# Cross attention's output projection: batches 0 with 1 and 2 with 3 in seven block products instead of eight

## The chip, the cores and the metric

The kernel runs on one core of one Trainium2 chip. The metric is the device time of one launch in microseconds (us): the median of three runs. Besides there is one profiled execution, whose trace gives the start and the duration of every instruction on TensorE (PE, matmuls), VectorE (DVE), ScalarE (ACT), GpSimd (POOL) and SyncE (SP, which here issues nearly all DMAs), and the DMA transfers.

## The reference

A decoder of two layers with the norm behind each residual add, in float32, on `x` of 8 batches of 128 tokens with 512 features. It has a self-attention, a cross attention on a context of the same shape, and feed-forward parts with routed experts and low-rank factors. The part that the change touches is the second layer's cross attention. For each batch, cut to what matters:

```python
hidden = concat([ctx, x])                     # 256 rows of 512
q = x @ Wq.T; k = hidden @ Wk.T; v = hidden @ Wv.T   # 16 query heads, 4 key heads, of 96
p = softmax(q @ k.T / sqrt(96))               # four query heads share a key head
o = p @ v                                     # 128 tokens x 1536 features
x = layernorm(x + o @ Wo.T)                   # Wo.T: 1536 x 512
```

The product `o @ Wo.T` is the output projection. Behind it stands the low-rank feed-forward `f1` of the same batch with its own residual add and norm, and the result goes to `out`.

## The kernel before, in words

All work of the last stage (from about 500 us on) is one loop, `for b in range(B): for hh in range(2)`. Each pass works on eight of the 16 heads of one batch:

- `Heads8` issues 48 score matmul instructions (`s_x`), DVE takes the maxima (`m_x`), ACT the exponentials (`e_x`), DVE scales and transposes blocks of 32x32 (`exps`).
- `turn` moves the transposed blocks into place with 16 DMAs of 64 KB on SP's queue, `pT_x<-e_x`. The tile pT has one buffer, so the moves of batch b wait until `o_x` of batch b-1 has read it. `e_x` has two buffers.
- `outputs(b)`, through `mixed`, multiplies by the values: 48 matmul instructions in three groups (`o_x`), each group in a PSUM bank of its own, whose copy to `oT` frees the bank.
- `projected(b)` does the projection, twelve float32 matmuls that are two instructions each, so 24 instructions of 128x512 (`pox`, line 998), with the three weight tiles `w_X_o`, and `add_norm` adds the residual and norms on DVE, with one power on POOL.
- `low_rank(b - 1)` issues steps of the f1 part: `low_tokens` (transposes), `low_scores`, `low_turn` and `low_last` of several batches, each a pass later.

PE's gaps are filled by `Front`: queries, keys and values of the next two batches in 14 pieces; `nxt.go(n)` issues the next n. PE, SP and the other queues run in program order. The order is written out by hand by this loop; the tile framework adds the semaphores. Matmul outputs share four PSUM banks of one tag. The last two batches have an order of their own, with moves on SP's and ACT's queues, and the last projection in two halves of 256 columns (line 1225).

The weight pool has eight slots of 1 MB. The three `w_X_o` tiles (in_X_o0, o1, o2) are loaded at about 462 to 502 us, ahead of the stage:

```python
wos = [weight(f"X_o{i}").rearrange("p (c o) -> p c o", c=4) for i in range(3)]
```

and the pass order around the change is:

```python
if b < B - 2 and hh == 0:
    nxt.go((4, 3)[j] if b < B - 3 else 2)
    if b:
        mix(b - 1)            # outputs(b - 1), projected(b - 1)
    pTs[b] = pT_tile(b)
    now.turn(pTs[b])
```

Of the kernel before, what the change touches and what calls it, by code (L numbers as in the profile page):

```python
# [11 lines left out]
F32 = mybir.dt.float32  # L12
AF = mybir.ActivationFunctionType
ALU = mybir.AluOpType
# [3 lines left out]
P = 128  # L18
B, S, D = 8, 128, 512
# [24 lines left out]
def decoder(ctx: ExitStack, tc: tile.TileContext, a: dict, out: bass.AP):  # L44
    nc = tc.nc

    glob = ctx.enter_context(tc.tile_pool(name="glob", bufs=1))
    xp = ctx.enter_context(tc.tile_pool(name="xp", bufs=10))
    wp = ctx.enter_context(tc.tile_pool(name="wp", bufs=8))
# [13 lines left out]
    def weight(key):  # L63
        src = a[key]
        t = wp.tile([P, 2048], F32, tag="w", name=f"w_{key}")
        n = src.shape[1]
        nc.sync.dma_start(t[:, :n], src)
        return t
# [212 lines left out]
    xs = [None] * B  # L281
# [6 lines left out]
    ap = attn.enter_context(stage("a0", 2))  # L288
# [232 lines left out]
    for n, (p, f) in enumerate(steps):  # L521
# [8 lines left out]
        now = Heads16(ap, units, causal_bias, oTs[p][:, :, f, :], f"a0_{p}_{f}")  # L530
# [244 lines left out]
    ap = layer.enter_context(stage("a1", 2))  # L775
# [10 lines left out]
    NS = XD // 32  # L786
# [65 lines left out]
    for b in range(B):  # L852
        qT, kbd = qk
        v_now = v
        oT = ap.tile([P, NC, P], F32, tag="oT", name=f"oT1_{b}")
        for f in (0, 2):
# [4 lines left out]
            now = Heads16(ap, units, alibi_bias(f), oT[:, f : f + 2, :], f"a1_{b}_{f}", keys_late)  # L861
# [46 lines left out]
    layer.close()  # L908
    for k in ("q0", "q1", "q2"):
        wqs.append(weight4(f"X_{k}"))  # L910
    wos = [weight(f"X_o{i}").rearrange("p (c o) -> p c o", c=4) for i in range(3)]


    with stage("x1b", 2, side="right") as ap, stage("f1", 2, side="right") as fp:
# [9 lines left out]
        class Heads8:  # L924
# [42 lines left out]
            def turn(self, pT, queues=(nc.sync,)):  # L967
                e = self.e.rearrange("p (s j) h k -> p s j (h k)", s=2)
                for i in range(4):
                    for j in range(4):  # L970
                        queues[j % len(queues)].dma_start(
                            pT[32 * j : 32 * j + 32, :, i, self.h0 // 2, :], e[32 * i : 32 * i + 32, :, j, :]
                        )

# [17 lines left out]
        def projection(b, oT, between={}):  # L992

            po = bank(f"pox_{b}")
            for i in range(NX):
                n, h = divmod(i, G)
                w = wos[(h * NS + n) // 4][:, (h * NS + n) % 4, :]
                nc.tensor.matmul(po, lhsT=oT[:, n, h * P : (h + 1) * P], rhs=w, start=(i == 0), stop=(i == NX - 1))  # L998
                for piece in between.get(i, ()):
                    piece()  # L1000
            return po

        def turned_low(b):
            xT = fp.tile([P, NC, P], F32, tag="xT", name=f"xTf1_{b}")
# [72 lines left out]
        nxt, upcoming = Front(1), None  # L1077
        tokens_low, scores_low, turned_lows = {}, {}, {}

        def low_tokens(b):  # L1080
            tokens_low[b] = turned_low(b)

        def low_scores(b):
            scores_low[b] = scored(b, tokens_low.pop(b))

        def low_turn(b):
            turned_lows[b] = turned_heads(b, scores_low.pop(b))

        def low_last(b):
            last(b, low_sum(b, turned_lows.pop(b)))  # L1090

        def low_rank(b):

            if b >= 2:
                low_turn(b - 2)
            if b >= 1:
                low_scores(b - 1)
            low_tokens(b)
            if b >= 2:
                low_last(b - 2)  # L1100

        def pT_tile(b):
            return ap.tile([P, 2, 4, 2, 8 * 32], F32, tag="pT", name=f"pT_x1_{b}", bufs=1)

        pTs, vs_x, oTs_x = {}, {}, {}

        def outputs(b):
            oTs_x[b] = ap.tile([P, NS, 512], F32, tag="oT", name=f"oTx_{b}", bufs=1)
            mixed(b, vs_x.pop(b), pTs.pop(b), oTs_x[b])

        def projected(b, between={}):
            po = projection(b, oTs_x.pop(b), between)
            xs[b] = add_norm(xs[b], po, f"x1_{b}")

        def mix(b):
            outputs(b)
            projected(b)

        for b in range(B):
            pr, j = divmod(b, 2)  # L1120
            if j == 0 and b:
                front, nxt = nxt, upcoming
            toks = slice(j * P, (j + 1) * P)
            for hh in range(2):
                now = Heads8(front.qT[:, :, toks], front.kT[:, :, :, toks], 2 * hh, f"x1_{b}_{hh}")
                now.maxima()
                now.exps(0)
                now.exps(1)
                if b < B - 2 and hh == 0:

                    nxt.go((4, 3)[j] if b < B - 3 else 2)
                    if b:
                        mix(b - 1)
                    pTs[b] = pT_tile(b)
                    now.turn(pTs[b])
                elif b < B - 2:
                    if j == 1 and b < B - 3:

                        upcoming = Front(pr + 2)
                    now.turn(pTs[b])  # L1140
                    nxt.go(2)
                    if b:
                        low_rank(b - 1)
                    if b < B - 3:
                        nxt.go((1, 2)[j])
                elif hh == 0:

                    if b == B - 2:
                        front.go(3)
                    else:  # L1150
                        projected(b - 2)
                    first = now
                else:
                    low_turn(b - 3)
                    outputs(b - 1)
                    if b == B - 2:
                        low_scores(B - 4)
                        low_last(B - 5)
                    else:
                        low_tokens(B - 3)  # L1160

                    pTs[b] = pT_tile(b)
                    for heads in (first, now):
                        heads.turn(pTs[b], (nc.sync, nc.scalar))
            vs_x[b] = front.v[:, j]
# [40 lines left out]
        b = B - 1  # L1206
        oT = oTs_x.pop(b)
# [12 lines left out]
        for half, cols in enumerate(halves):  # L1220
            po = bank(f"pox_{b}_{half}")
            for i in range(NX):
                n, h = divmod(i, G)
# [102 lines left out]
def _rows(w):  # L1326

    return np.ascontiguousarray(w.T.reshape(-1, P, w.shape[0]).transpose(1, 0, 2)).reshape(P, -1)


def _layouts(i):
    x, c = i["x"], i["ctx_4096"]
    xT = x.reshape(B // 2, 2 * P, NC, P).transpose(3, 0, 2, 1)
    cT = c.reshape(B // 2, 2 * S, NC, P).transpose(3, 0, 2, 1)
    wqkv = i["L1_attn_Wqkv"]
    cols = lambda v: v.reshape(NC, P).T
    HG = E0 * R0 // 2
    lora_b = np.zeros((P, 2 * D), np.float32)
    lora_b[:HG] = i["L0_ffn_lora_B"].transpose(0, 2, 1).reshape(2, HG, D).transpose(1, 0, 2).reshape(HG, 2 * D)
    a = {  # L1340
        "x": x,
        "xT": xT,
        "ctx": c,
        "ctxT": cT,
        "masks": _mask_table(),
        "dft": _dft_table(),
        "alibi": _alibi_table(),
        "vecs": np.stack(
            [cols(i[k]) for k in ("L0_attn_bq", "L0_attn_bk")], axis=1
        ),  # L1350
        "L1_lnq": np.stack([cols(i[f"L1_attn_{k}"]) for k in ("q_ln_w", "q_ln_b")], axis=1),
        "L1_ln": np.stack([i[f"L1_attn_{k}"] for k in ("q_ln_w", "q_ln_b", "k_ln_w", "k_ln_b")]),
        "L0_bvo": np.stack([i["L0_attn_bv"], i["L0_attn_bo"]]),
        "F0_base": _rows(i["L0_ffn_base_W"]),
        "F0_lora": np.concatenate(
            [_rows(np.concatenate([i["L0_ffn_gate_W"], i["L0_ffn_lora_A"].reshape(E0 * R0, D)])), lora_b], axis=1
        ),
        "F1": np.concatenate(
            [
                _rows(np.concatenate([i["L1_ffn_Wr"], i["L1_ffn_A"].reshape(H1 * R1, D)])),  # L1360
                i["L1_ffn_B"].transpose(0, 2, 1).reshape(H1 * R1, D),
            ],
            axis=1,
        ),
        "F1_br": i["L1_ffn_br"],
        "L1_Wo": _rows(i["L1_attn_Wout"]),
        "X_v": _rows(i["L1_xattn_Wv"]),
    }
    for n in "qkvo":
        a[f"L0_W{n}"] = _rows(i[f"L0_attn_W{n}"])  # L1370
        if n in "qk":
            a[f"L0_W{n}"] = a[f"L0_W{n}"].reshape(P, NC, NC, P).transpose(0, 2, 1, 3)
    for n, j in zip("qkv", range(3)):
        a[f"L1_W{n}"] = _rows(wqkv[j * D : (j + 1) * D])

    NS = XD // 32
    wq = i["L1_xattn_Wq"].reshape(KV, G, NS, 32, D).transpose(1, 2, 0, 3, 4).reshape(3, 512, D)
    wo = i["L1_xattn_Wo"].reshape(D, KV, G, NS, 32).transpose(0, 2, 3, 1, 4).reshape(D, 3, 512)
    for j in range(3):
        a[f"X_q{j}"] = _rows(wq[j])  # L1380
        a[f"X_o{j}"] = _rows(wo[:, j])
    a["X_k"] = _rows(i["L1_xattn_Wk"].reshape(KV, NS, 32, D).transpose(1, 0, 2, 3).reshape(KV * XD, D))
    return {k: np.ascontiguousarray(v) for k, v in a.items()}

# [17 lines left out]
```

## Time and profile before

| | |
|---|---|
| median of 3 runs | 873.94 us (873.93 to 873.97) |
| profiled execution, its own time | 874.61 us |
| its span | 872.8 us |
| PE busy in the span | 847.6 us (97%) |
| DVE, ACT, POOL busy | 542.3, 365.1, 202.7 us |
| DMA | 50.67 MB, mean 58 GB/s |

The profile's page and the views of the trace count from the start of the span. A line of a view names the engine, the source line (L998 is line 998), the tiles it writes and reads (`pox<-w_X_o,oTx`), the number of instructions (x24), and durations. "SPq" is SP's queue of DMA issues. PEclk is the clock granted to TensorE, 1.00 being full speed. Matmuls overlap, so the busy time of a single one is longer than the distance between two.

### The profile page before, as it was taken

What the parts mean: (1) busy time and instruction counts of PE and PEld (TensorE: products, weight loads), DVE (VectorE), ACT (ScalarE), POOL (GpSimd) and SP (SyncE); (2) the same over time, 40 slices, a digit from 0 to 9 for tenths busy, and PEclk for the clock granted to TensorE, in tenths of its full rate; (3) what the DMA queues carried; (4) which work ended last, traced back from release to release, by engine and by line L of the source; (5) the groups of instructions that cost most, each with busy time, mean ns of one, the idle gap of its engine ahead of it and who ended that gap; (6) DMA issues with size and microseconds to landing.
All of it is one profiled execution on the core that took longest, in us unless ns stands there. A gap on an engine that the chain in (4) does not pass through costs nothing.

```text
span 872.8 us, 17973 instructions
## 1 busy us (share of the span) xinstructions
PE 847.6 (97%) x6482; PEld 525.3 (60%) x6482; DVE 542.3 (62%) x2214; ACT 365.1 (42%) x1527; POOL 202.7 (23%) x299
## 2 busy tenths in 40 slices
PE   9999999999899999999999999999999999999996
PEld 5776655655454455555555587848385846576454
DVE  3656687777868667777778413724372546467654
ACT  3886574654222136766666403304031322224310
POOL 2500243242535314555555300000000000000000
PEclk9999999999999999999999999999999999999999
DMA  9700000130300002000003020432213211313340
GB/s 327 310 2 26 2 13 14 50 110 10 137 13 0 25 0 98 2 2 2 2 3 145 26 74 1 88 82 49 46 36 86 44 46 36 82 41 80 84 93 36
DMA packets 30073, 50.67 MB, mean 58 GB/s; under 512 B 5536, under 2 KB 22048, under 8 KB 28192
## 3 DMA queue, kind: packets, MB, share of 16 engines
q1 hardware_dynamic: 27424, 47.42, 18.0%
q10 hardware_dynamic: 2560, 2.10, 1.1%
q8 instruction: 51, 0.84, 0.4%
q14 instruction: 38, 0.31, 0.1%
HBM read 30.63 MB, written 2.10 MB: 37 GB/s over the span
## 4 chain that ended last, share of the span: by engine, by line
PE 64%; DVE 18%; ACT 11%; POOL 3%; issue 1%; DMA 1%; ACTq 0%; SPq 0%; POOLq 0%; DVEq 0%
PE pqx L86 10%; PE pox L998 7%; ACT e_a L197 7%; PE pkx L86 4%; PE pvx L86 4%; PE s_x L936 4%; PE o_x L981 4%; PE pq L86 3%; PE pk L86 3%; DVE e_a L184 3%; PE pv L86 3%; PE po L86 3%; PE pt_a L228 2%; PE pof L623 2%; PE s_a L165 2%
## 5 line engine op out<-in xcount | busy, mean ns | idle before, releaser
L197 ACT ACTIVATE e_a<-e_a,m_a 128x128 f32<-128x128 f32 (+1 forms) x512 | 184.7, 364 | 98.7 <-DVE m_a L184 98.7
L957 ACT ACTIVATE e_x<-s_x,m_x 128x256 f32<-128x256 f32 x128 | 58.7, 484 | 139.6 <-DVE m_x L947 122.5
L197 ACT ACTIVATION_READ_ACCUMULATOR e_a<-e_a,m_a 128x1 f32 x512 | 97.0, 189 | 0.0
L86 PE MATMUL pqx<-xTx,w_X_q 128*128 128x256 f32 x384 | 84.9, 380 | 0.0
L86 PEld LDWEIGHTS pqx<-xTx,w_X_q 128*128 128x128 f32 x384 | 72.6, 190 | 11.4 <-issue 1.8
L998 PE MATMUL pox<-w_X_o,oTx 128*128 128x512 f32 x168 | 74.1, 596 | 0.7 <-DVE oTx L987 0.6
L97 POOL TENSOR_TENSOR rs_x<-ve_x,neghalf 128x1 f32<-128x1 f32 x7 | 3.9, 550 | 268.5 <-DVE ve_x L95 249.4
L946 DVE TENSOR_REDUCE m_x<-s_x 128x4 f32<-128x1024 f32 x32 | 37.6, 1218 | 41.5 <-PE s_x L936 41.5
L211 POOL TENSOR_TENSOR e_a<-e_a,rc_a 128x512 f32<-128x512 f32 (+1 forms) x64 | 52.8, 847 | 33.8 <-DVE rc_a L208 18.8
L998 PEld LDWEIGHTS pox<-w_X_o,oTx 128*128 128x128 f32 x168 | 31.3, 190 | 40.9 <-issue 39.2
L228 PE MATMUL pt_a<-ident,e_a 128*128 128x128 f32 x384 | 48.4, 273 | 2.3 <-DVE m_a L184 2.3
L936 PE MATMUL s_x<-kTx,qTx 32*128 32x256 f32 x768 | 50.0, 385 | 0.6 <-ACT e_x L957 0.6
L228 PEld LDWEIGHTS pt_a<-ident,e_a 128*128 128x128 f32 x384 | 43.4, 140 | 11.2 <-issue 4.7
L184 DVE CUSTOM_DVE_ANT_0 e_a<-s_a,masks 128x128 f32<-128x128 f32 (+1 forms) x256 | 46.8, 253 | 4.5 <-PE s_a L165 3.1
L936 PEld LDWEIGHTS s_x<-kTx,qTx 32*128 32x128 f32 x768 | 39.0, 184 | 16.7 <-issue 11.7
L184 DVE CUSTOM_DVE_ANT_0 e_a<-s_a,alibi 128x128 f32<-128x128 f32 (+1 forms) x256 | 47.3, 252 | 1.4 <-PE s_a L165 1.3
L981 PE MATMUL o_x<-pT_x,vx 128*32 128x512 f32 x384 | 43.7, 595 | 1.9 <-DVE mv_x L93 0.7
L184 DVE DVE_READ_ACCUMULATOR2_ANT m_a<- 128x1 f32 x512 | 42.5, 83 | 0.0
L965 DVE STREAM_TRANSPOSE e_x<-e_x 128x1024 f32<-128x1024 f32 x32 | 39.7, 1241 | 0.8
L964 DVE TENSOR_SCALAR e_x<-e_x,rc_x 128x256 f32<-128x256 f32 x128 | 36.3, 347 | 3.5 <-DVE rc_x L961 2.3
L165 PEld LDWEIGHTS s_a<-kbd,qT 32*64 32x64 f32 x1024 | 20.9, 131 | 27.9 <-issue 15.4
L103 DVE TENSOR_TENSOR x_x<-pox,x_a 128x512 f32<-128x512 f32 x7 | 4.8, 686 | 52.5 <-PE pox L998 52.5
(236 smaller groups left out, 1625.4 us busy)
## 6 DMA issues: line engine op xcount, KB each, us to landing
pT_x<-e_x SPq DMA_DIRECT2D x224, 64.0 KB, 2.0
w_X_q<-in_X_q SPq DMA_DIRECT2D x3, 1024.0 KB, 4.9
w_X_o<-in_X_o SPq DMA_DIRECT2D x3, 1024.0 KB, 4.9
w_L_Wv<-in_L_Wv SPq DMA_DIRECT2D x2, 1024.0 KB, 6.6
w_L_Wo<-in_L_Wo SPq DMA_DIRECT2D x2, 1024.0 KB, 7.5
x_in<-in_x SPq DMA_DIRECT2D x8, 256.0 KB, 7.5
ct<-in_ctx SPq DMA_DIRECT2D x8, 256.0 KB, 2.7
cT<-in_ctxT SPq DMA_DIRECT2D x4, 512.0 KB, 3.9
```

The lines of the kernel that those rows point to most:

```text
L86: nc.tensor.matmul(ps, lhsT=l, rhs=r, start=(i == 0), stop=(i == n - 1))
L165: nc.tensor.matmul(s[r // 2][64 * u : 64 * u + 64, r % 2, cols], lhsT=qT[rows, 64 - 64 * part : P - 64 * part], rhs=kbd[rows, :, :keys], s ...
L184: self.scored = nc.vector.tensor_tensor_reduce(self.e[:, r, cols], s[i][:, r % 2, cols], bias(r, cols), -1.0, 3e38, ALU.add, ALU.min, self ...
L197: nc.scalar.activation(e[:, r, x, :], e[:, r, x, :], AF.Exp, scale=-1.0, bias=self.m[:, part, r, x : x + 1], accum_out=self.su[:, part, r, ...
L211: nc.gpsimd.tensor_tensor(e, e, bc(self.rc[:, part, rs, :].unsqueeze(3), list(e.shape)), ALU.mult)
L228: nc.tensor.transpose(pt[:, r, cols], self.e[:, 2 * i + r, cols], ident)
L936: nc.tensor.matmul(sc[g // 2][:, g % 2, u * 256 : (u + 1) * 256], lhsT=qT[rows, (h0 + u) * NS + n, :], rhs=kT[rows, n], start=(n == 0), st ...
L946: nc.vector.tensor_reduce(m, self.s[i], AX.X, ALU.max, negate=True)
L957: nc.scalar.activation(self.e[:, :, j, :], self.s[half][:, i, :].rearrange("p (a k) -> p a k", k=32), AF.Exp, bias=self.m[:, j : j + 1], s ...
L965: nc.vector.transpose(self.e[:, :, js, :], self.e[:, :, js, :])
L981: nc.tensor.matmul(po[32 * g : 32 * g + 32, :], lhsT=v[:, s, g * XD + 32 * n : g * XD + 32 * n + 32], rhs=pT[:, s].rearrange("p i h x -> p ...
L998: nc.tensor.matmul(po, lhsT=oT[:, n, h * P : (h + 1) * P], rhs=w, start=(i == 0), stop=(i == NX - 1))
```

## The change

For the batches 0 and 1, and again 2 and 3, the two projections are done together. Stacked, the two batches' `o` is a matrix of two block rows (batches) and two block columns (768 features each), and Wo.T one of two by two blocks of 768 x 256. The product of two by two blocks is formed in seven block products and a number of block sums (Winograd's form) instead of eight products. One block product is six matmuls of 128x256, two instructions each, so a pair has 84 instructions of 128x256 where there were 48 of 128x512. Batches 4 to 7 are projected as before.

- The weight sums: `form_sums` loads three tiles of 1 MB (in_X_ot) behind the moves of batch 0's first half, and POOL forms the sums in place with twelve subtractions of 128x512. `keep_sums`, behind the moves of batch 0's second half, writes them to a tensor `ts` in DRAM (3 MB). The early load of `w_X_o` is gone.
- `stream(t)` loads one slot's worth (1 MB, in one or two DMAs) of blocks and kept sums, in the order in which the products read them. `stream(0)` to `stream(2)` stand behind the moves of batch 1's first half. Inside a pair, after every eight matmuls, the slot just used is loaded anew; `plain_outputs` loads the plain weights behind the second pair.
- In `paired` POOL forms the left sums, ACT copies two products out of PSUM, DVE and POOL add the products and the residual, and both batches are normed.
- `oT` has two buffers. For even b up to 4 the pass has three front pieces, `outputs`, one piece, `paired`; for odd b the projection is missing from the pass.
- The low-rank steps of batches 0 to 4 are issued from a table `LOWS`, later than before, and the tail has `low_turn` and `low_last` of one more batch.

```diff
-    wos = [weight(f"X_o{i}").rearrange("p (c o) -> p c o", c=4) for i in range(3)]
+    slots = [wp.tile([P, 2048], F32, tag="w", name=f"w_X_o_{i}") for i in range(3)]
+    wos = [t.rearrange("p (c o) -> p c o", c=4) for t in slots]
+    kept = ctx.enter_context(tc.tile_pool(name="kept", bufs=1, space=bass.MemoryType.DRAM))
+    weight_sums_kept = kept.tile([P, 4, 3, 512], F32, tag="ts", name="ts")
+    def form_sums():
+        for i, t in enumerate(slots):
+            nc.sync.dma_start(t, a["X_ot"][:, i])
+            b11, b12, b21, b22 = (t[:, j * 512 : (j + 1) * 512] for j in range(4))
+            nc.gpsimd.tensor_tensor(b11, b12, b11, ALU.subtract)
+            nc.gpsimd.tensor_tensor(b12, b22, b12, ALU.subtract)
+            nc.gpsimd.tensor_tensor(b22, b22, b11, ALU.subtract)
+            nc.gpsimd.tensor_tensor(b21, b21, b22, ALU.subtract)
+    def keep_sums():
+        for i, t in enumerate(slots):
+            nc.sync.dma_start(weight_sums_kept[:, :, i, :], t.rearrange("p (j o) -> p j o", j=4))
...
+    BLOCK = 6 * 256
+    ORDER = [B11, T1, B21, T2, B22, T3, T4]
+    def stream(t):
+        lo, hi = 2048 * t, min(2048 * (t + 1), 7 * BLOCK)
+        while lo < hi:
...
+            nc.sync.dma_start(slots[t % 3][:, lo - 2048 * t : lo - 2048 * t + n], source[:, base + off : base + off + n])
+            lo += n
+    def plain_outputs():
+        for i, t in enumerate(slots):
+            nc.sync.dma_start(t, a[f"X_o{i}"])
...
-                        queues[j % len(queues)].dma_start(
+                        self.moved = queues[j % len(queues)].dma_start(
...
+        def paired(b0, b1):
+            o0, o1 = oTs_x.pop(b0), oTs_x.pop(b1)
...
+            def product(left):
+                ps = bank(f"pox_{b0}_{used[0]}")[:, :256]
+                for kk in range(6):
+                    h, n = divmod(kk, NS)
+                    t, u = divmod(used[0], 8)
+                    nc.tensor.matmul(
+                        ps, lhsT=left[:, n, h * P : (h + 1) * P], rhs=slots[t % 3][:, u * 256 : (u + 1) * 256],
+                        start=kk == 0, stop=kk == 5,
+                    )
+                    used[0] += 1
+                    if u == 7:
+                        if t < 3:
+                            stream(t + 3)
+                        elif t < 5 and not paired.last:
+                            stream(t - 3)
+                return ps
+            add(nc.gpsimd, s, o1[:, :, first], o1[:, :, second])
+            add(nc.gpsimd, o1[:, :, first], o0[:, :, first], o1[:, :, first], ALU.subtract)
+            nc.scalar.copy(p1, product(o0[:, :, first]))
+            nc.scalar.copy(p5, product(s))
+            add(nc.gpsimd, s, s, o0[:, :, first], ALU.subtract)
+            add(nc.gpsimd, x0[:, first], x0[:, first], p1)
+            add(nc.vector, r0[:, first], product(o0[:, :, second]), x0[:, first])
+            add(nc.gpsimd, o0[:, :, second], o0[:, :, second], s, ALU.subtract)
+            add(nc.vector, p1, product(s), p1)
+            add(nc.gpsimd, x0[:, second], x0[:, second], p5)
+            add(nc.gpsimd, x0[:, second], x0[:, second], p1)
+            add(nc.vector, r0[:, second], product(o0[:, :, second]), x0[:, second])
+            add(nc.gpsimd, x1[:, second], x1[:, second], p5)
+            add(nc.vector, p1, product(o1[:, :, first]), p1)
+            add(nc.gpsimd, x1[:, first], x1[:, first], p1)
+            add(nc.gpsimd, r1[:, second], x1[:, second], p1)
+            add(nc.vector, r1[:, first], product(o1[:, :, second]), x1[:, first])
+            if paired.last:
+                plain_outputs()
+            else:
+                stream(2)
...
-            oTs_x[b] = ap.tile([P, NS, 512], F32, tag="oT", name=f"oTx_{b}", bufs=1)
+            oTs_x[b] = ap.tile([P, NS, 512], F32, tag="oT", name=f"oTx_{b}", bufs=2)
...
+        PAIRED = 4
+        LOWS = {
+            2: [lt(0), lt(1)],
+            3: [lsc(0), lsc(1)],
+            4: [lh(0), lh(1), lt(2), ll(0), lt(3), ll(1)],
+            5: [lsc(2), lsc(3), lt(4)],
+        }
...
-                    nxt.go((4, 3)[j] if b < B - 3 else 2)
-                    if b:
+                    if b > PAIRED:
+                        nxt.go((4, 3)[j] if b < B - 3 else 2)
                         mix(b - 1)
+                    elif b and not j:
+                        nxt.go(3)
+                        outputs(b - 1)
+                        nxt.go(1)
+                        paired.last = b == PAIRED
+                        paired(b - 2, b - 1)
+                    else:
+                        nxt.go((4, 3)[j])
+                        if b:
+                            outputs(b - 1)
                     pTs[b] = pT_tile(b)
                     now.turn(pTs[b])
+                    if b < 2:
+                        with tc.issue_after(now.moved.ins):
+                            if b:
+                                for t in range(3):
+                                    stream(t)
+                            else:
+                                form_sums()
                 elif b < B - 2:
...
                     now.turn(pTs[b])
+                    if not b:
+                        with tc.issue_after(now.moved.ins):
+                            keep_sums()
                     nxt.go(2)
-                    if b:
-                        low_rank(b - 1)
+                    for piece in LOWS.get(b, ()):
+                        piece()
```

## The prediction

> **What bounds the kernel.** The page first: TensorE (PE) is busy 97% of the span, and its idle time there is small. So what counts is PE work removed, and any place where PE is made to wait.
>
> ```profile
> PE 847.6 (97%) x6482; PEld 525.3 (60%) x6482; DVE 542.3 (62%) x2214; ACT 365.1 (42%) x1527; POOL 202.7 (23%) x299
> ```
>
> Second, the chain of waits for 565 to 660 us (start, us, what; cross attention of batches 0 to 2):
>
> ```profile
> 570.28 5.29 PE o_x L981 x48
> 575.57 10.50 PE pox L998 x24
> ...
> 614.89 1.90 PE o_x L981 x16
> ...
> 617.56 1.97 PE o_x L981 x16
> ...
> 620.24 1.97 PE o_x L981 x16
> ...
> 622.84 10.57 PE pox L998 x24
> ...
> 653.27 6.91 PE pqx L86 x32
> ```
>
> A projection is 24 instructions of 128x512 in 10.50 us: 0.4375 us each. A 128x256 one costs 6.91/32 = 0.216. Batch 1's o_x is cut into three: each third waits until its accumulator's copy has given the one free PSUM bank back.
>
> Third, the timeline of SP's queue (start, us) from 545 to 611 us, in pieces: the moves of each half of pT, the context load between, the halves of batch 1.
>
> ```profile
> 546.12 10.33 SPq L971 DMA_DIRECT2D pT_x<-e_x  x16
> 557.41 10.68 SPq L971 DMA_DIRECT2D pT_x<-e_x  x16
> 568.18 0.53 SPq L800 DMA_DIRECT2D cT<-in_ctxT  x1
> 575.63 10.70 SPq L971 DMA_DIRECT2D pT_x<-e_x  x16
> 598.90 10.67 SPq L971 DMA_DIRECT2D pT_x<-e_x  x16
> ```
>
> Sixteen moves take 10.3 to 10.7 us of SP (0.64 each) and land 2.0 later. The last of batch 0 is issued at 567.5 and lands near 569.5; o_x of batch 0 starts at 570.28, when PE's queries end. The slack is 0.7 us. So SP's queue is the second bound.
>
> Fourth, what large loads and long waits cost: the page's issues, those of 20 to 40 us (four 1 MB loads in a row), and the windows around PE's wait at 225.5 us (us, PE busy, PEclk, DMA, GB/s).
>
> ```profile
> pT_x<-e_x SPq DMA_DIRECT2D x224, 64.0 KB, 2.0
> w_X_o<-in_X_o SPq DMA_DIRECT2D x3, 1024.0 KB, 4.9
> w_L_Wo<-in_L_Wo SPq DMA_DIRECT2D x2, 1024.0 KB, 7.5
> ```
>
> ```profile
> w_F_base<-in_F_base SPq DMA_DIRECT2D x1, 1024.0 KB, 7.8
> w_L_Wk<-in_L_Wk SPq DMA_DIRECT2D x1, 1024.0 KB, 13.2
> ```
>
> ```profile
> 225.50:228.20 2.70, 0.08 (x1) 0.96 0.02 9
> 228.20:229.20 1.00, 0.97 (x5) 0.50 0.00 0
> 229.20:230.20 1.00, 1.00 (x3) 0.50 0.00 0
> ```
>
> A 1 MB load alone lands in 4.9 us. Of four issued 0.67 apart the first lands 7.8 and the last 13.2 after its issue: (13.2+3x0.67-7.8)/3, about 2.5 us per MB. After 2.65 us of idle PE the granted clock was 0.50 until 231.4, 3.4 us.
>
> **What the change removes.** (a) Each of two pairs: 48 instructions of 128x512 (21.0 us) become 84 of 128x256 (84 x 0.2168 = 18.2). Two pairs: -5.6 us.
>
> (b) For even b the order is now three front pieces, `outputs`, one piece, product. The fourth piece held banks; without it two are free. Batch 1's o_x took 622.84-614.82 = 8.02 us; 5.36 are its matmuls and 0.70 moved-up scores, so 1.96 is stall. Batch 3's at 706.6 is the same. I take back 1.96 and 1.1 (there a bank is still held by low-rank work): -3.1; bounds 0 and -3.9.
>
> **What it adds on SP, part one (stall A).** Between batch 0's two groups of moves come three 1 MB loads of `form_sums`, issued 556.5 to 557.8. By the w_X_o row and 2.55 per MB they land near 561.4, 564.0, 566.5. In the changed kernel's order every SP issue waits for the issue eight before it. So move 6 of the second group waits for load 1, move 8 for load 3 (566.5), and moves 9 to 16 follow at 0.64: last issue 571.7, landing 573.7. PE wants it at 570.25: 3.4 us of idle, nothing else being ready on PE, whose queue is in order. Bounds: 0.3 if loads and moves share the engines so well that only three issues (1.9, less the slack and the gap of 1.0 between the groups) are felt; 5.5 if the loads land as at 23 us, first after 7.8. I take 3.4, by the w_X_o row, whose loads are like these in size. The twelve Pool instructions (128x512 with two tensors: 1.27 us, L478) start at 561.4 and end near 577, beside all this; the third write of `keep_sums` waits for them, and behind it on SP stand the context load and batch 1's moves, gated by o_x until 579 anyhow: nothing. After 3.4 us of idle I charge the clock as after 2.65: 3.4 us at half, 1.7 us; bounds 0 and 1.7.
>
> [...]
>
> **Part two (stall B).** Let T be the end of batch 0's o_x. Batch 1's first moves take T to T+10.9, six `stream` loads (3 MB) to T+14.7. The last of these lands near T+20.7 (start T+10.9, fixed part 2.0 as the moves show, 3 x 2.55). The second group's move 8 waits for it; move 16 goes at T+25.9 and lands T+27.9. With the projection gone from this place PE reaches o_x of batch 1 at T+2.8+13.9+2.8+1.0+5.2 = T+25.7 (scores, queries, scores, transposes, two thirds of the values). Stall 2.2 us; the bounds are 1.1, where only the six issues are felt (second group from T+14.7 instead of T+12.9, where its softmax ends), and 5, where the loads land as at 23 us. Without the loads the last move would land at T+25.0, just in time. A clock fall here: 0 to 1.7, at nothing, as 2.2 is under the 2.65 seen.
>
> **Inside a pair.** Pool's subtractions of 128x768 (1.27 x 1.5 = 1.9 us) are chained; the fifth product's left side needs the second product's end (5.2 us into the pair), a subtraction, two 128x256 adds of 0.65 and another subtraction: 5.2+1.9+1.3+1.9 = 10.3, and some 0.3 for semaphores, against the product's start at 10.4. So 0.2 late per pair: 0.4 for both pairs; bounds 0 and 2. A slot is consumed in 8 x 2 x 0.2168 = 3.47 us, so a stream has 6.9 us from issue to use against 4.9 + 0.6: covered with 1.4. Batch 4's o_x is limited by its moves already (0.6 wait before); the pair's DVE work adds 0.7 (bounds 0 and 2).
>
> **Later.** The low-rank steps of batches 0 to 3 move by the LOWS table; their PE work is the same. One more add and norm (f1 of batch 2) falls to DVE in the tail, where the chain runs DVE, ACT's queue, pT, e_x (808.31 to 813.06 us in the trace): add 0.59, statistics 0.70 and scaling 0.55 are 1.8, of which I let 1.0 reach the end, since some of it falls into a wait of 0.65 there; bounds 0 and 2.5. Leaving out the early 3 MB loads at 462 us saves nothing: they hide.
>
> **Sum.** -5.6 -3.1 +3.4 +1.7 +2.2 +0.4 +0.7 +1.0 = +0.7. The profiled execution took 874.6 with a span of 872.8, 0.7 over the median 873.94; a difference of spans carries over: 874.6 us. With each term at its bounds the mechanism holds some 870 to 878.
>
> **Rival 1, faster: the stalls are hidden.** If loads and moves interleave on the DMA engines, A is near 0.3 with no clock fall, and B 1.1: -8.7+0.3+1.1+2.1 = -5.2, so 868.7; with B at 0, 867.6. For it: a move is 64 KB and moves alone use under half the DMA engines (0.41 from 575.6 to 586.1 us). Against: the wait for the issue eight before holds moves whatever their size. It decides at pT landing before 570.3. [...]
>
> **Rival 2, slower: streams late inside the pair.** Place: streams 3 and 4, issued behind a PE release and read 6.9 us later. The w_L_Wo row has 1 MB landing after 7.5, w_F_base 7.8, the next 9.6. With 7.5 to 9.6 the stall is 7.5+0.6-6.9 = 1.2 to 3.3 per pair, 2.4 taken: +4.8, so 879.4. For: the streams come in pieces, partly from the sums in DRAM, and the next 1 MB is issued 3.5 behind. Against: at 2.5 us per MB the engines keep up. It decides at a landing of 6.3.
>
> That the sums bring no saving in PE time at all (128x256 matmuls at more than 0.22) is spoken against by L1225's tail products of that form.
>
> **Chances.** Forecast 0.50 (870 to 878), rival 1 0.20, rival 2 and stalls at their upper bounds 0.30. 0.2% is 1.75 us, about what a measurement can tell. Within the forecast 0.10 of the 0.50 falls under 872.2, 0.22 between, 0.18 above 875.7. Faster 0.30, same 0.22, slower 0.48. The range 867 to 881 leaves out about a tenth at either end.
>
> **What would show it.** Right: the pox products at 0.217 each, 168 of them; PE idle 3 to 4 us before o_x of batch 0 and PEclk 0.5 after it; a second wait of some 2 us before o_x of batch 1; o_x of batches 1 and 3 in one run; SP waits on w_X_o loads ahead of pT moves. Wrong: no PE idle there (rival 1), or pox waiting on a DMA of w_X_o (rival 2), or DVE and Pool slowing each other in the pairs.

## The result, and the profile after

The changed kernel takes 881.23 us (median of 6 runs, 879.55 to 883.60) against 873.96 (873.71 to 874.70): a ratio of 1.0084, interval 1.0068 to 1.0100. It is slower by 7.3 us. The forecast was 874.6 with a range to 881.0, so the time lies just outside. The profiled execution took 881.59, its span is 879.8, 7.0 more than before.

The page first, PE's line and the landing times of the new DMAs:

```profile
PE 843.9 (96%) x6554; PEld 539.8 (61%) x6554; DVE 551.1 (63%) x2220; ACT 366.6 (42%) x1531; POOL 240.8 (27%) x331
```

```profile
w_X_o<-in_X_ot SPq DMA_DIRECT2D x3, 1024.0 KB, 8.2
...
w_X_o<-in_X_ob SPq DMA_DIRECT2D x4, 768.0 KB, 4.6
w_X_o<-ts SPq DMA_DIRECT2D x6, 512.0 KB, 5.5
```

PE's busy time fell by 3.7 us, and yet the span grew by 7.0: PE waits. Where, the timeline of SP's queue tells (start, us):

```profile
556.18 1.56 SPq L917 DMA_DIRECT2D w_X_o<-in_X_ot  x3
557.85 16.86 SPq L1008 DMA_DIRECT2D pT_x<-e_x  x16
574.81 2.86 SPq L926 DMA_DIRECT2D ts<-w_X_o  x3
...
583.34 10.92 SPq L1008 DMA_DIRECT2D pT_x<-e_x  x16
594.31 0.59 SPq L942 DMA_DIRECT2D w_X_o<-in_X_ob  x1
```

Batch 0's second group of moves took 10.68 us of SP before; now it takes 16.86, behind the three loads. The chain of waits for 534 to 700 us goes through just these places:

```profile
557.31 11.69 DMA w_X_o<-in_X_ot
...
574.12 2.01 DMA pT_x<-e_x
...
576.26 7.06 PE o_x L1018 x48
...
596.90 10.47 DMA w_X_o<-ts
...
612.49 2.00 DMA pT_x<-e_x
...
614.69 8.28 PE o_x L1018 x48
...
625.75 18.29 PE pox L1056 x84
```

The third load holds the chain for 11.69 us, then nine moves go out one by one, then o_x starts at 576.26 (before: 570.28), and takes 7.06 us instead of 5.29. The same happens again with the streams and batch 1's moves. PE's waits (total us, times, longest) around batch 0's, batch 1's and batch 4's o_x, and SP's from 555 to 615 us:

```profile
PE o_x L1018 <- DMA pT_x<-e_x: 6.7, 1, 6.7
PE o_x L1018 <- DMA pT_x<-e_x: 5.6, 1, 5.6
PE o_x L1018 <- DMA pT_x<-e_x: 0.7, 1, 0.7
```

```profile
SPq L1008 <- DMA w_X_o<-in_X_ot: 6.7, 2, 3.4
SPq L1008 <- DMA w_X_o<-ts: 4.3, 2, 3.0
```

So SP itself waited 6.7 us for the loads. In the trace the DMAs take eight semaphores in turn, and each of these issues went out only when the DMA eight issues before it had landed: move 6 of the group at 561.05, load 1 having landed at 561.03, move 7 at 565.07 (load 2: 565.05), move 8 at 569.01 (load 3: 569.00). The seven moves issued ahead of that had landed by 570.34, so what o_x waited for is the nine behind. In and behind both stalls the granted clock (last columns: PEclk, DMA share, GB/s) is 0.50, from 572.84 to 579.66 and from 613.80 to 620.62:

```profile
569.00:573.00 4.00, 0.57 (x3) 0.98 0.35 78
573.00:577.00 4.00, 0.74 (x4) 0.50 0.58 162
577.00:581.00 4.00, 4.00 (x32) 0.67 1.03 380
...
613.00:617.00 4.00, 2.31 (x12) 0.60 0.15 33
617.00:621.00 4.00, 4.00 (x24) 0.55 0.00 0
```

The pair itself does what it says: 84 products in 18.29 us and, for the second pair, 18.31, with no wait for weights.

### The profile page after: what moved, and what is told of

Its sections match the earlier page's. It is cut to its first block, busy times and chain, and to the rows that moved or that the text cites. A ratio compares the mean times of both kernels' runs of the same rounds, so it can differ in the third digit from the quotient of the medians.

```text
span 879.8 us, 18232 instructions
## 1 busy us (share of the span) xinstructions
PE 843.9 (96%) x6554; PEld 539.8 (61%) x6554; DVE 551.1 (63%) x2220; ACT 366.6 (42%) x1531; POOL 240.8 (27%) x331
## 2 busy tenths in 40 slices
DMA packets 35258, 67.99 MB, mean 77 GB/s; under 512 B 5984, under 2 KB 22496, under 8 KB 32992
## 4 chain that ended last, share of the span: by engine, by line
PE 55%; DVE 20%; ACT 10%; SPq 5%; DMA 4%; POOL 3%; issue 2%; ACTq 0%; POOLq 0%; DVEq 0%
PE pqx L86 7%; ACT e_a L197 6%; SPq L1008 5%; PE pox L1056 4%; PE o_x L1018 4%; PE pq L86 4%; DVE e_a L184 3%; PE pk L86 3%; PE pv L86 3%; PE po L86 3%; PE s_x L973 3%; PE pkx L86 2%; PE pt_a L228 2%; PE pox L1035 2%; PE pof L623 2%; PE pvx L86 2%
## 5 line engine op out<-in xcount | busy, mean ns | idle before, releaser
L211 POOL TENSOR_TENSOR e_a<-e_a,rc_a 128x512 f32<-128x512 f32 (+1 forms) x64 | 52.8, 846 | 35.1 <-DVE rc_a L208 18.8
L1018 PE MATMUL o_x<-pT_x,vx 128*32 128x512 f32 x384 | 47.6, 646 | 14.1 <-DMA pT_x<-e_x 13.0
L973 PE MATMUL s_x<-kTx,qTx 32*128 32x256 f32 x768 | 46.6, 383 | 0.0
L1001 DVE TENSOR_SCALAR e_x<-e_x,rc_x 128x256 f32<-128x256 f32 x128 | 42.6, 395 | 3.9 <-DMA pT_x<-e_x 2.6
L1018 PEld LDWEIGHTS o_x<-pT_x,vx 128*32 128x32 f32 x384 | 13.3, 117 | 44.0 <-issue 33.6
L843 ACT COPY qTx<-pqx 128x512 f32<-128x512 f32 x24 | 14.2, 592 | 55.9 <-PE pqx L86 55.9
L165 PE MATMUL s_a<-kbd,qT 32*64 32x256 f32 (+1 forms) x1024 | 33.5, 334 | 1.5 <-ACT pT_a L229 1.0
L1048 POOL TENSOR_TENSOR s_x<-oTx 128x768 f32<-128x768 f32 x2 | 3.6, 1810 | 113.1 <-DVE oTx L1024 113.1
```

Of the source, the lines that this page charges most:

```text
L165: nc.tensor.matmul(s[r // 2][64 * u : 64 * u + 64, r % 2, cols], lhsT=qT[rows, 64 - 64 * part : P - 64 * part], rhs=kbd[rows, :, :keys], s ...
L211: nc.gpsimd.tensor_tensor(e, e, bc(self.rc[:, part, rs, :].unsqueeze(3), list(e.shape)), ALU.mult)
L973: nc.tensor.matmul(sc[g // 2][:, g % 2, u * 256 : (u + 1) * 256], lhsT=qT[rows, (h0 + u) * NS + n, :], rhs=kT[rows, n], start=(n == 0), st ...
L1001: nc.vector.tensor_scalar(e, e, self.rc[:, j : j + 1], None, ALU.mult)
L1018: nc.tensor.matmul(po[32 * g : 32 * g + 32, :], lhsT=v[:, s, g * XD + 32 * n : g * XD + 32 * n + 32], rhs=pT[:, s].rearrange("p i h x -> p ...
```

## The experiments

Two theories were tested. **Q**: the loss is made at SP's queue, by moves of pT that stand behind large loads. **P**: the pair itself costs, by Pool and DVE slowing each other, by streams inside the pair, by more DMA traffic.

**Sums early (e1).** The sums' loads and subtractions where the plain weights were loaded before; the rest as changed.

```diff
+    form_sums()                      # behind plain_outputs, ahead of the stage
...
-                    if b < 2:
+                    if b == 1:
                         with tc.issue_after(now.moved.ins):
-                            if b:
-                                for t in range(3):
-                                    stream(t)
-                            else:
-                                form_sums()
+                            for t in range(3):
+                                stream(t)
```

> Weight sums loaded and formed where the plain weights were loaded before (about 462 to 510 us); the writes to DRAM and the streams stay where the change has them. Theory Q (moves of pT held on SP behind the large loads): the wait ahead of batch 0's o_x (6.75 us in the changed kernel) and the half clock after it (1.66) go, the wait ahead of batch 1's o_x (5.7) stays: 881.2 - 8.4 + 0.7 (the shift that the missing early loads gave) = 873.5 us. Rival P (the pair itself costs: Pool and DVE slowing each other, streams inside the pair, more DMA traffic): 879 or more.

Measured 876.22 us (874.10 to 878.83; before 874.24), ratio 1.0023 (1.0012 to 1.0034), 2.7 above the expectation; run e3 below shows where such a loss comes from. Batch 0's wait is gone, batch 1's is there:

```profile
PE o_x L1019 <- DMA pT_x<-e_x: 6.4, 1, 6.4
```

**Streams late (e2).** The first three streams behind batch 1's second group instead of its first.

```diff
-                            if b:
-                                for t in range(3):
-                                    stream(t)
-                            else:
-                                form_sums()
+                            form_sums()          # only for b == 0
...
-                    if not b:
+                    if b < 2:
                         with tc.issue_after(now.moved.ins):
-                            keep_sums()
+                            if b:
+                                for t in range(3):
+                                    stream(t)
+                            else:
+                                keep_sums()
```

> The first three streams moved behind the second group of moves of batch 1, all else as changed. Theory Q: the wait ahead of batch 1's o_x (5.7 us) and the half clock after it (about 1.7) go, that of batch 0 stays: 881.2 - 7.4 = 873.8 us, with o_x of batch 1 some 1.2 shorter still if its copies then keep up. Rival P: 879 or more, or the first product now waits for its weights (then 876).

Measured 875.02 us (874.12 to 875.80), ratio 1.0007 (0.9998 to 1.0016), 1.2 above the expectation; 0.6 of it is a longer wait ahead of batch 4's o_x (1.3 against 0.7 in the changed kernel). Now batch 1's wait is gone and batch 0's stands:

```profile
PE o_x L1018 <- DMA pT_x<-e_x: 6.8, 1, 6.8
```

**Both (e3).** The two edits together.

> Both edits: sums formed early, first streams behind the second group of moves of batch 1. Theory Q: both waits gone, 881.2 - 8.4 - 7.4 + 0.7 = 866.1 us, 0.991 of before: the saving of 5.2 in the products and of 1 to 2 in the thirds of o_x is then seen. Rival P: 875 or more.

Measured 868.57 us (868.30 to 868.72), ratio 0.9935 (0.9920 to 0.9950). Neither large wait is left; of waits for pT there is only batch 4's:

```profile
PE o_x L1019 <- DMA pT_x<-e_x: 0.9, 1, 0.9
```

This is theory Q: the same pairs, the same 3 MB of sums and the same streams inside the pairs, and 12.7 us less. It is 2.5 above the expectation. The timeline of POOL (this kernel, then one line of the kernel before) and PE's windows of 465 to 500 us (us, busy; this kernel, then the kernel before) tell where:

```profile
466.81 1.27 POOL L674 TENSOR_TENSOR k<-k,lnv 128x512 f32<-128x512 f32 x1 [1.33 <-DVE k L672]
468.05 1.27 POOL L919 TENSOR_TENSOR w_X_o<-w_X_o 128x512 f32<-128x512 f32 x1
469.29 1.26 POOL L675 TENSOR_TENSOR k<-k,lnv 128x512 f32<-128x512 f32 x1
...
471.86 1.27 POOL L921 TENSOR_TENSOR w_X_o<-w_X_o 128x512 f32<-128x512 f32 x1
473.08 1.61 POOL L211 TENSOR_TENSOR e_a<-e_a,rc_a 128x512 f32<-128x512 f32 x2
```

```profile
469.57 1.61 POOL L211 TENSOR_TENSOR e_a<-e_a,rc_a 128x512 f32<-128x512 f32 x2
```

```profile
465.00:500.00 35.00, 32.36 (x350) 1.00 0.16 58
```

```profile
465.00:500.00 35.00, 34.40 (x375) 1.00 0.17 60
```

The subtractions (L919 to L921) stand between Pool's steps for self-attention (L674, L675, L211), which before followed each other; e_a comes 3.5 us later, and PE loses 2.0 us there.

**The loads alone, without the change (e4).** The kernel before; only its three output weight loads stand behind batch 0's first moves.

```diff
-    wos = [weight(f"X_o{i}").rearrange("p (c o) -> p c o", c=4) for i in range(3)]
+    slots = [wp.tile([P, 2048], F32, tag="w", name=f"w_X_o_{i}") for i in range(3)]
+    wos = [t.rearrange("p (c o) -> p c o", c=4) for t in slots]
...
                     now.turn(pTs[b])
+                    if not b:
+                        with tc.issue_after(now.moved.ins):
+                            plain_outputs()
```

> The kernel before, its eight products and its order unchanged; only the three 1 MB loads of the plain output weights stand behind batch 0's first group of moves instead of at 462 to 502 us. Theory Q: the wait ahead of batch 0's o_x appears here too, about 6 to 7 us, with 1.7 of half clock after it: 874.0 + 8.4 - 0.7 = 881.7 us. Rival P: under 1 us of wait, 874 to 875.

Measured 883.32 us (882.91 to 884.49), ratio 1.0103 (1.0086 to 1.0120): the stall without any pair, sum or stream. SP's timeline shows the picture of the changed kernel:

```profile
545.59 10.84 SPq L976 DMA_DIRECT2D pT_x<-e_x  x16
556.48 1.57 SPq L916 DMA_DIRECT2D w_X_o<-in_X_o  x3
558.15 17.11 SPq L976 DMA_DIRECT2D pT_x<-e_x  x16
```

```profile
PE o_x L986 <- DMA pT_x<-e_x: 7.1, 1, 7.1
```

PE waited 7.1 us, and o_x took 8.2 instead of 5.3 at half clock. That is 1.2 longer than in the changed kernel and most of the 1.6 by which the time is above the expectation.

**One load (e6), two loads (e7).** The same with one or two of the three loads moved, the others early.

```diff
+    plain_outputs(range(2))          # e7: range(1)
...
-                            plain_outputs()
+                            plain_outputs(range(2, 3))   # e7: range(1, 3)
```

> The kernel before with one of the three 1 MB output weight loads behind batch 0's first group of moves, the other two early as before. Theory Q: move 8 waits for the load, which lands near 561.4, before that move's own turn at 562.5; the last move lands 0.6 later, no wait of over 0.3: 874.0 to 874.5 us. A theory by which any large load among the moves costs in proportion (a third of e4's 9): 877.

> The same with two of the three loads. Theory Q: move 8 waits for load 2, near 564 on most DMA engines and 565.2 on the last one; the last move lands 571.2 to 572.4, PE waits 1.0 to 2.4 us; half clock after it 0 to 1.7: 875 to 878. In proportion: 880.

Measured for one load 874.94 us (before 874.52), ratio 1.0007 (0.9997 to 1.0016), a wait of 0.3; for two 880.51, ratio 1.0068 (1.0053 to 1.0083):

```profile
PE o_x L988 <- DMA pT_x<-e_x: 0.3, 1, 0.3
```

```profile
PE o_x L988 <- DMA pT_x<-e_x: 4.0, 1, 4.0
```

One MB costs nothing that the runs can tell, the second 5.6 us: not in proportion, as Q says, since move 8 waits only if the load is not there by its own turn. It is the one-load run that speaks against proportion (877 expected by it); the two-load time by itself is what proportion expected (880). And for Q the two-load wait is 1.6 above the upper end of what was expected, and o_x took 2.8 longer. In the trace load 2 has landed on half of the 16 DMA engines by 563.9 and on the last one at 566.26; move 8 was issued at 566.28, 0.02 after that last one. The expectation had 565.2 for that engine.

**The loads from another queue (e8).** The kernel before, the three loads issued by ACT behind batch 0's second exponentials.

```diff
-            nc.sync.dma_start(t, a[f"X_o{i}"])
+            nc.scalar.dma_start(t, a[f"X_o{i}"])
...
                     now.turn(pTs[b])
+                    if not b:
+                        with tc.issue_after(now.exped.ins):   # last exponential of this half
+                            plain_outputs()
```

> The kernel before with its three output weight loads issued by ACT behind batch 0's second exponentials (553 to 555 us) instead of by SP. In this order SP's moves 6, 7 and 12 of the second group still wait for the loads' semaphores. If the semaphore waits alone hold the moves: moves 1 to 5 land about 2 us after issue, move 12 waits for load 3 (566 to 568), the last one lands 571 to 573: a wait of 1 to 3 us, 876 to 878. If the loads hold the moves on the DMA engines whatever queue they are on: moves 1 to 5 land only with the loads, near 564 and later.

Measured 879.76 us (877.92 to 881.38), ratio 1.0059 (1.0041 to 1.0077), a wait of 3.4 us. The line of pT's tile from 555 to 573 us:

```profile
DMA to landing us min/median/max: 2.0/4.1/7.5
```

The moves on SP's queue landed with ACT's loads: issued at 553.55 and 554.19 they landed at 560.48 and 562.16, load 2 at 561.83. So the moves are late twice over: these two took 6.9 and 8.0 us to land, though the loads were on another queue, and behind them SP waited 5.1 us for landings (4.3 for moves, 0.8 for a load). (ACT's third load itself went out only at 562.5.) The time is 1.8 above the range that was expected if the semaphores alone held the moves. It is also 3.6 below e4, but two of the loads were issued 3.4 us sooner here, so the two runs do not tell what the queue is worth. No run changed the number of semaphores, so the shares of the two causes stay open. The two moves landed 2.1 and 0.3 us after the load that had been issued ahead of them, where a move by itself takes 2.0 from its issue.

**The order alone (e9).** The kernel before with the changed order of the pass for batches 2 and 4, and plain projections.

```diff
-                    nxt.go((4, 3)[j] if b < B - 3 else 2)
-                    if b:
-                        mix(b - 1)
+                    if b and not j:
+                        nxt.go(3)
+                        outputs(b - 1)
+                        nxt.go(1)
+                        projected(b - 1)
+                    else:
+                        ...
```

> The kernel before with the changed order alone for batches 2 and 4: three front pieces, o_x of the batch before, one piece, its plain projection; no pair, no loads moved. It prices the second gain of the prediction by itself. By the prediction (1.96 and 1.1 us of stall gone): 874.0 - 3.1 = 870.9 us. By the changed kernel's trace, where o_x of batch 3 still took 6.22 us instead of 5.29 (before: 8.02 with 0.70 of scores inside): 2 x 1.1 = 2.2 gone, 871.8. If the order of the pieces brings nothing: 874.

Measured 870.78 us (870.58 to 871.49; before 874.17), ratio 0.9961 (0.9947 to 0.9975): 3.4 us gained, the prediction's 3.1 rather than the 2.2 read from the changed kernel's trace. The chain of waits:

```profile
615.70 1.92 PE o_x L981 x16
617.62 2.78 PE pvx L86 x8
620.40 10.30 PE pox L998 x24
```

The piece of values behind o_x now covers its copies, which before stood in front of the projection. But o_x of the batches 1 and 3 still takes 6.29 and 6.24 us here, so only 1.0 and 1.1 of the 1.96 us of stall went from each; the other 1.3 of the 3.4 came behind o_x.

**Sums after self-attention (e5).** As e3, but the sums are loaded, formed and written between 510 and 533 us, when Pool and SP have nothing to do.

```diff
+            self.loaded = nc.sync.dma_start(self.cT, a["ctxT"][:, pr])
...
         nxt, upcoming = Front(1), None
+        with tc.issue_after(nxt.loaded.ins):
+            form_sums()
+            keep_sums()
```

> As the run with both edits, but the sums' loads, Pool's twelve subtractions and the three writes to DRAM stand behind the context load at about 510 us, when Pool has done its last work for self-attention and SP has nothing to move until 545. Theory Q: in the run with both edits Pool's subtractions between 468 and 484 us delayed self-attention by 2.2 us on PE; that goes: 868.6 - 2.2 = 866.4 us. If instead the delay came from the loads themselves: 868 to 869.

Measured 865.92 us (865.75 to 867.50; before 874.52), ratio 0.9906 (0.9890 to 0.9923). The expected 866.4 was 0.5 too high. The first pair in its chain of waits:

```profile
609.88 18.29 PE pox L1056 x84
```

It beats both kernels: the change pays 8.6 us when its 9 MB of loads and writes ahead of the first pair stand where no move waits behind them.

## Why the prediction was wrong

The mechanism and the places were right; two stalls were sized at half or less, and the half clock after the second was put at nothing. Its terms against the measured ones, in us:

| term | predicted | measured |
|---|---|---|
| (a) products, with what is late inside a pair | -5.6 + 0.4 | 18.29 + 18.31 - 4 x 10.5 = -5.4; e5 against e9, each from its own before: -8.6 + 3.4 = -5.2 |
| (b) o_x in thirds | -3.1 | -3.4 (e9) |
| stall A | +3.4 | +6.7 |
| half clock after A | +1.7 | 7.06 - 5.29 = +1.8 |
| stall B | +2.2 | +5.6 |
| half clock after B | 0 | 8.28 against 6.3 in e3 = +2 |
| batch 4's o_x | +0.7 | 0.7 of wait against 0.6 = +0.1 |
| tail | +1.0 | from batch 4's o_x to the end 122.3 before and after = 0 |

The measured terms make +7.4; the spans differ by 7.0, the profiled execution being 0.7 us ahead already at 532 us. That is variation of a run and no gain from leaving out the early loads: 0.4 of it is there at 11 us, and e9, which has these loads, is 0.9 ahead at the same place.

Term (b) came near by some luck: the prediction took back 1.96 and 1.1 us of the stall inside o_x, e9 gave 1.0 and 1.1 there, and 1.3 behind o_x that the prediction did not name.

**Stall A** failed in one step, the landing of load 3. The worked-out 566.5 was right for the median DMA engine (566.25 in the trace) and fifteen of 16 engines had it by 566.8; the last one landed at 569.00, and move 8 was issued at 569.01. From there the working holds: eight more moves at 0.64, the last issued at 574.12, landing at 576.1 instead of 573.7. The remaining 0.75 is that PE was ready at 569.5, not 570.25. The upper bound, taken from loads that queue behind other loads, is given as 5.5, but its own parts make 6.1: 556.5 + 7.8 + 2 x 2.47 = 569.2 for load 3, eight more moves and a landing make 576.4, against 570.25. Counted from the same 570.25 the measured stall is 6.0. That is near by luck: in those rows the first load was late already, while here load 1 landed after 4.9 us, as in the w_X_o row, and it is one engine's part of load 3 that came late.

**Stall B** is the same step, the landing of the last load: T was 583.3, the last stream was worked out for T+20.7 (its parts make T+20.55), so for 604.0. Half of the engines had it at 605.0, the last at 607.4, here with the engines spread out and not one far behind the others (the last two are 0.3 apart). And since the stall came out at 5.6 instead of 2.2, the half clock that was left out for lack of idle time came too; the reason given, that 2.2 is under 2.65, would not have held either, as the last section shows. These three sizes make up the miss: 3.3 + 3.4 + 2.0 = 8.7 of it, with 1.6 of cost that did not come (tail, batch 4) on the other side. The range of 870 to 878 is not the sum of the terms at their bounds, as it is said to be: those add up to -8.1 and +14.8, which is 866 to 889.

**Rival 1** (loads and moves interleave) is refuted: the moves issued at 557.85 and 558.48 landed at 569.20 and 569.40, after load 3 on the same queue (569.00); in e8, with the loads on another queue, moves took up to 8.0 us. **Rival 2** (streams late inside the pair) is refuted for the place named: streams 3 and 4 of the first pair had landed by 633.5 and 638.0, and were read from 636.0 and 639.6. What the prediction has the change remove, -8.7, is what e5 measures (-8.6): of the 2.1 of other costs next to nothing came.

That Pool and DVE slow each other in the pairs, or that traffic costs by itself (theory P), no run supports: e5 moves the same 67.99 MB and the pair takes 18.29 us there as well.

## What to carry to other kernels

A large load did not just take DMA time here: on a queue with small moves behind it, it held their issue too (SP waited 6.7 us for the loads in the changed kernel), since with this program's eight semaphores no issue went out before the one eight ahead of it had landed, and the nine moves left then went out one by one, 0.64 us each, on the critical path. So before putting a load behind a group of moves, count from the load's last landing, on the slowest DMA engine, the issues still to come and their landing, against when the consumer wants them; or put the load where the queue has nothing to move, as between 510 and 545 us here. With the stalls of 3.4 (e8) to 7.1 us (e4) the granted clock also fell to 0.50, so their price was more than the wait: o_x took 1.7 (e8) to 2.9 us (e4) longer.

## What the runs showed of the hardware

**The half clock comes in steps.** From the clock columns of the windows, the time at half clock (lost share times window, doubled) is, by the wait ahead of it: 3.4 us after 2.65 (kernel before, at 225 us) and after 3.4 (e8), 6.8 after 4.0 (e7), 5.6 and 6.7 (changed kernel), 6.4 (e1) and 6.8 (e2), 10.2 after 7.1 (e4); none after 0.3 (e6) and 0.9 (e3). For e8 and e7 the lines are these:

```profile
569.00:573.00 4.00, 0.58 (x7) 1.00 0.52 105
573.00:577.00 4.00, 4.00 (x24) 0.57 0.30 115
```

```profile
569.00:573.00 4.00, 0.51 (x3) 0.92 0.48 104
573.00:577.00 4.00, 3.46 (x20) 0.50 0.42 132
577.00:581.00 4.00, 4.00 (x32) 0.73 0.00 0
```

(1 - 0.57) x 4 x 2 = 3.4, and (0.08 + 0.50 + 0.27) x 4 x 2 = 6.8. Only the part behind the wait costs.

The length of the wait alone does not decide it. At 225 us the same wait of 2.65 us as in the kernel before is followed by full clock in e1 and e5, and one of only 2.1 to 2.2 us is followed by 3.4 us at half clock in e6 to e9. The stretch behind the wait, first of e5 (2.65 us of wait), then of e6 (2.17):

```profile
227.75:231.20 3.45, 3.44 (x13) 1.00 0.00 0
```

```profile
227.96:231.37 3.41, 3.41 (x5) 0.50 0.00 0
```

In the traces of the kernel before and of the changed kernel the stretches between two changes of the clock are whole multiples of 3.41 us: 221.87 (65 times), 3.41 and 638.29 (187) before; 221.87, 3.41, 341.33 (100), 6.83 (2), 34.13 (10), 6.83 and 256.00 (75) in the changed kernel. By these steps, PE's idle time in a step that was followed by one at half clock was 2.42 us in the kernel before (from 224.59), and 3.27, 3.41 (from 569.43), 3.41 and 0.89 (from 610.39) in the changed kernel. What decides whether a wait is followed by half clock is not shown: no run moved a wait against the steps.

The changed kernel's runs spread over 4 us (before: 1 us); that the clock makes this spread was not tested.

**One DMA engine of 16 is late.** In the stretch of 556 to 570 us of the changed kernel (busy share in 40 slices, then the queue of instruction loads) the engines are nearly full up to 567 us (32 slices of 0.35), and then their share drops below a tenth while load 3 still has not landed:

```profile
DMA  5363993999999899999899989989899942000000
...
q8 instruction: 1, 0.02, 0.4%
```

That packet is a load of 16 KB of instructions, 0.97 us long, at 561.3. Such a packet lies in the same stretch of e2, e4 and e7 too, where the last engine was 1.7 to 2.5 us behind the one before it. In the kernel before, with no load near, a packet of 0.93 us at 559.09 goes with a move (issued at 558.04) whose last engine landed 1.07 us behind the one before. In e3 the first streams, without such a packet, landed on the last engine within 0.3 us of the one before. That this load is the cause is not shown: its 0.97 us are less than half of the 2.2 us of delay, and no run moved it.
